# A fused attention and feed-forward block: dense work dealt to the attention steps in unequal shares, one diagonal to a part, values one step later

## The chip, the cores and the metric

The kernel runs on one core of a Trainium2 chip. The metric is the device time of one launch in microseconds (us). Three runs of the kernel before gave 3266.70, 3270.58 and 3273.54 us; their median is 3270.58.

## The reference

The input x has 16 batches of 512 tokens of width 512, in float32. Each batch passes through one block:

```python
a = attention(layernorm(x))           # 32 heads of width 16, biases, rotary positions, causal softmax
x = x + layernorm(a @ Wo.T + bo)
y = layernorm(x)
h = silu((y @ gate_w.T) * gate_s) * ((y @ up_w.T) * up_s)     # 1408 wide, weights are -1, 0 or 1
x = x + layernorm((h @ down_w.T) * down_s)
```

The layernorms have no parameters.

## The kernel before, in words

**Two strands in one program.** The attention is cut into head groups of four heads. A batch b has eight groups, and group n = 8b + g takes five *steps*, i = 0 to 4. After the attention matmuls of a step, a *share* of dense work is put into the program: projections, output projection, gate, up and down products, layernorms and transposes of the batch before and the batch after. `one_step` writes this order down. Each engine keeps the order of the program (`InOrder`), so the order written out is the order in which every engine's queue runs.

**A step of attention** (`one_step`, `scores`). A step issues two kinds of score matmuls into the two PSUM tiles `sc` (two heads in each):

- The transposed scores (keys on partitions) of group n, one part of `ST_PARTS`, go into the lower half. The row maxima are subtracted by a third matmul with `mx`. ScalarE takes the exponential of each tile into `pa` or `pc` (`weights`), and GpSimd clears the upper triangle of a diagonal block there.
- The plain scores (queries on partitions) of a group ahead, one part of `S_PARTS`, go into the upper half. VectorE adds a causal mask where the part holds a diagonal block, and reduces to the negated row maxima `nm` (`maxima`). Part = (i + 3) mod 5, so part 0 falls in step 2.

The two engines go through the tiles crosswise: ScalarE takes the first tile while VectorE takes the second, and then they change. The next step's scores write the same two tiles. In step 2 the finished maxima are transposed by TensorE (`turn_maxima`, PSUM tile `pm`) and split in two pieces (`nmh`, `nml`), which are written to `mx`.

**Values.** `values(n, 0)` multiplies the first weights `pa` (made in steps 0 and 1) by v, at the end of step 2 of the same group. `values(n, 1)` does the rest at the end of step 0 of the next group, and ScalarE copies the result out as `ot`. In a profile they are the matmuls `av`: 8 and 24 records.

**Dense work.** `dense`, `gate_ups` and `downs` build a list of items (cost, function). A float32 matmul costs `MM` = 1.0, an fp32r matmul `M1` = 0.27 and a transpose `TR` = 0.15; loads and vector work cost nothing. The functions are:

- `product`: a block of matmuls into one PSUM tile of a pool of three; the last matmul's item also calls the `tail`, which reads the tile on ScalarE or VectorE.
- `qk_block`: four matmuls; the tail makes `ys` (ScalarE, twice) and `ya` (VectorE), `rest` adds them (VectorE), makes the rounded piece `yh` (ScalarE) and the remainder `yl` (GpSimd). There is one buffer `ya`.
- `o_block`, `gate_up`, `down`: output projection (`po`), gate and up (`pg`, `pu`, each 8 fp32r matmuls) and down (`pd`, 22 fp32r matmuls to a token block). `split` makes the pieces `hh` (ScalarE) and `hl` (GpSimd) of the hidden values for the down product, with two buffers each; it stands in the list behind every eighth down matmul.
- `turn`: four transposes into one PSUM tile `px`.
- `merge` puts a piece of work in "after so many units of cost"; `laid` resolves this.

A full batch's list runs: v (16 matmuls), q (16), output projection (16), k (16) with transposes between, gate and up of 11 slices, and four down blocks with transposes. It has about 140 units for 40 steps. Batch 0 runs beside a shorter list (`first_list`, 46 steps, about one matmul a step), batch 14 beside one without down products, batch 15 beside a mixed one; the last dense work (`last_list`) has no attention beside it.

**How it is dealt out** (`run_list`). Each step takes items until the work done reaches an equal fraction of the total:

```python
goal = total * (s + 1) / steps
while i < len(L) and (done + L[i][0] / 2 < goal or s == steps - 1):
```

Loads are issued on SyncE's queue by items of the lists or by `later`.

Of the kernel before, what the change touches and what calls it, by code (L numbers as in the profile page):

```python
# [13 lines left out]
ALU = mybir.AluOpType  # L14
# [21 lines left out]

HALF = T // 2
ST_PARTS = [[(0, 0, 256, 0)], [(0, 256, 256, 0)], [(1, 128, 256, 0)], [(1, 384, 128, 0), (3, 384, 128, 128)], [(2, 256, 256, 0)]]
S_PARTS = [[(3, 0, 256, 0)], [(3, 256, 256, 0)], [(2, 0, 256, 0)], [(0, 0, 128, 0), (2, 256, 128, 128)], [(1, 0, 256, 0)]]
ST_DIAG = [0, None, 0, 128, 0]  # L40


class InOrder:
# [14 lines left out]
class Block:  # L58
# [54 lines left out]
    def constants(self):  # L113
        nc, a, con = self.nc, self.a, self.const
        for tb in range(NB):
            self.load_x(0, tb, ("x", "xr")[tb // 2], 2)
        ncol = sum(n for _, n in a["cols"][1])
        cols = con.tile([P, ncol], FP, tag="cols", name="cols")
        self.sp.dma_start(out=cols, in_=a["cols"][0])
        self.col, at = {}, 0  # L120
        for name, n in a["cols"][1]:
            self.col[name] = cols[:, at : at + n]
            at += n
        turn = con.tile([P, 2, T], FP, tag="turn", name="turn")
# [12 lines left out]
        self.row = {}  # L137
        for name in ("bo", "dscale"):
            self.row[name] = con.tile([P, C], FP, tag=name, name=name)
            nc.scalar.dma_start(out=self.row[name], in_=a[name].partition_broadcast(P))  # L140

        self.gh = con.tile([P, self.NF], FP, tag="gh", name="gh")
        self.gu = con.tile([P, self.NF], FP, tag="gu", name="gu")

        self.mask = con.tile([P, 2 * P], mybir.dt.bfloat16, tag="mask", name="mask")
        nc.gpsimd.memset(self.mask, 0.0)
        for i in range(2):
            m = self.mask[:, ts(i, P)]
            nc.gpsimd.affine_select(
                out=m, in_=m, compare_op=ALU.is_ge, fill=-BIG, base=0, pattern=[[-1, P]], channel_multiplier=1  # L150
            )
        self.sc = [self.ps_sc.tile([P, 2, T], FP, tag=f"sc{k}", name="sc") for k in range(2)]
        self.v17 = []
        for i in range(2):
            t = con.tile([P, NB, WIDTH], FP, tag=f"v17_{i}", name=f"v17_{i}")
            nc.gpsimd.memset(t, 0.0)
            nc.gpsimd.memset(t[:, :, DH : H * W : W], 1.0)
            self.v17.append(t)
        self.one = con.tile([P, P], FR, tag="one", name="one")
        nc.vector.memset(self.one.bitcast(FP), 1.0)  # L160
        self.qd, self.kd, self.od, self.rd = [], [], [], []
        for par in range(2):
            for c in range(NC):
# [110 lines left out]
        self.act.activation(out, src, AF.Identity, bias=mr[1], scale=mr[0])  # L274


    def turn(self, tiles, key, tb, to, big):

        st = {}

        def go(c):
            if c == 0:
                st["p"] = self.psum("px")
            self.pe.transpose(st["p"][:, ts(c, P)], tiles[key, tb][:, ts(c, P)], self.ident)
            if c == NC - 1:
# [12 lines left out]

        return [(TR, lambda c=c: go(c)) for c in range(NC)]

    def product(self, name, n, lhs, rhs, tail, cost=MM):
        st = {}

        def go(i):
            if i == 0:
                st["p"] = self.psum(name)
            self.pe.matmul(st["p"], lhs(i), rhs(i), start=(i == 0), stop=(i == n - 1))
            if i == n - 1:
                tail(st["p"])

        return [(cost, lambda i=i: go(i)) for i in range(n)]

    def norm_1(self, b, tb):
        xt = self.xts.pop((b, tb))
# [184 lines left out]
    def laid(items):  # L499
# [3 lines left out]
        for item in items:  # L503
# [2 lines left out]
                continue  # L506
            if item[0] == "need":
                for w in [w for w in waiting if w[2] == item[1]]:
                    out.append((0, w[1]))
                    waiting.remove(w)  # L510
                continue
            out.append(item)
            for w in waiting:
                w[0] -= item[0]
            for w in [w for w in waiting if w[0] <= 0]:
                out.append((0, w[1]))
                waiting.remove(w)
        return out + [(0, w[1]) for w in waiting]

    def dense(self, b, between=()):  # L520

# [105 lines left out]
    def maxima(self, m, part, s, two):  # L627
# [2 lines left out]
            self.nms[m] = self.tile([P, 2, 4, NB], "nm", bufs=2)  # L630
        full = self.nms[m]
        nm = full[:, :, two]
        if part in (1, 3, 4):
            d = s if part == 3 else s[:, :, P:HALF]
            mask = self.mask[:, 0 : d.shape[-1]].unsqueeze(1).to_broadcast(list(d.shape))
            self.dve.tensor_tensor(d, d, mask, ALU.add)
        out = [nm[:, 0, :, 3], nm[:, 1, :, 1], nm[:, 0, :, 2], nm[:, :, :, 0].rearrange("p x j -> p j x"), nm[:, 0, :, 1]][part]
        if part == 3:
            s = s.rearrange("p j (x t) -> p j x t", x=2)
        self.dve.tensor_reduce(out=out, in_=s, axis=AX.X, op=ALU.max, negate=True)  # L640
        if part == 4 and two.start == 0:
# [71 lines left out]
        self.later(2, lambda: self.pool.tensor_tensor(self.ocs[b, c], self.ocs[b, c], rc, ALU.mult))  # L713


    def run_list(self, L, steps):

        L = self.laid(L)
        total = sum(c for c, _ in L)
        done, i = 0.0, 0  # L720
        for s in range(steps):
            goal = total * (s + 1) / steps
            while i < len(L) and (done + L[i][0] / 2 < goal or s == steps - 1):
                L[i][1]()
                done += L[i][0]
                i += 1
            yield

    def gate_ups(self, o, nxt2, apart=False):
# [82 lines left out]
    def one_step(self, work, n, i):  # L812
# [5 lines left out]
        if i == 2 and 0 <= n + 1 < self.B * NG:  # L818
            self.turn_maxima(n + 1)
        next(work, None)  # L820
        if i == 2 and 0 <= n < self.B * NG:
            self.values(n, 0)
        if i == 0 and 0 <= n - 1 < self.B * NG:
            self.values(n - 1, 1)
# [2 lines left out]
    def front(self):  # L827
# [20 lines left out]
            return rest  # L848

        def turn(b, tb):  # L850
            for _, f in self.turn(self.xns, ("a", b), tb, self.xnts, ("xnta", "xntf")[b]):
                f()

        rest = None
# [14 lines left out]
        for name in "qk":  # L869
            for c in range(NC):  # L870
                items, rest, store = self.qk_block(0, name, c)
                for _, f in items[:2]:
                    f()
                for f in rests:
                    f()
                for _, f in items[2:]:
                    f()
                rests = [rest, store]
                if name == "q" and c == 0:
# [15 lines left out]
        nc.vector.tensor_scalar_mul(self.gh, self.col["gs"], 0.5)  # L895
        nc.vector.tensor_tensor(self.gu, self.gh, self.col["us"], ALU.mult)
        for tb in range(NB):
            for _, f in self.v_block(0, tb):
                f()
            if tb == 2:  # L900
                checks.pop(0)()
        for k in range(NC):
            self.wts[1, "v", k] = self.wts[0, "v", k]
        for tb in range(2):
            for _, f in self.v_block(1, tb):
                f()

    def first_list(self):
# [71 lines left out]

    def batches(self):
        B = self.B
        work = self.run_list(self.first_list(), 46)
        self.load_group(0)
        for n, i0 in ((-2, 2), (-1, 0)):
            for i in range(i0, STEPS):
# [16 lines left out]
        work = self.run_list(L + self.downs(B - 2, None, (0, 1), True, True), STEPS + 2)  # L1003
        for i in range(STEPS + 2):
            self.one_step(work, B * NG + i // STEPS, i % STEPS)
        for _, f in self.laid(self.last_list()):
            f()


# [59 lines left out]
```

## Time and profile before

| what | value |
|---|---|
| median of three runs | 3270.58 us |
| the profiled execution's own time | 3272.91 us |
| its span (first to last instruction) | 3271.1 us |
| PE (TensorE) busy | 3023.4 us, 92% |
| DVE (VectorE) busy | 2115.8 us, 65% |
| ACT (ScalarE) busy | 1607.1 us, 49% |
| POOL (GpSimd) busy | 1330.3 us, 41% |
| DMA queue of the loads and stores | 43.9% of 16 engines |
| mean granted TensorE clock | 0.979 |

Busy time is a union: matmuls overlap in the pipeline, so a busy PE is not an array at its peak. The number in a row of groups after "|" is the busy time and the mean of one instruction in ns, then the idle time of the engine just ahead of such instructions, and what ended it. In a timeline a row holds the start, the duration, engine, operation, output and inputs, the number of like instructions merged, and in brackets the idle time before them with what ended it. A float32 matmul of 512 columns appears as two records. All lines have the number L53, since a helper records every instruction; groups are told apart by the names of their tiles.

The timeline has batches 1 to 13 at 194 to 205 us each, batch 14 at 179 us. Before batch 0 the front part takes about 88 us, and the last dense work starts near 3140 us.

### The profile page before, as it was taken

Reading aid. Unit: us, or ns where it says so; the run is one execution under the profiler, and the core shown is the slowest. Engines: PE = TensorE matmul, PEld = TensorE weight load, DVE = VectorE, ACT = ScalarE, POOL = GpSimd, SP = SyncE. Lnnn points to the kernel's source line nnn. Section 1 sums busy time; section 2 is a strip of 40 time slices with the busy share of each in tenths; the row PEclk is TensorE's granted clock in tenths of the full one; section 3 lists DMA queues with packets and bytes.
Section 4 is the critical chain, followed back from the end, with each engine's and each line's share of the span. In section 5 each row is a group of like instructions: output and inputs, shape, how many; then the busy total and the mean of one; then the engine's idle time right before and its main releaser. Section 6 shows DMA issues by size and latency. Waiting matters only on the chain. (4 is left out here: it accounts for less than half of the span.)

```text
span 3271.1 us, 69062 instructions
## 1 busy us (share of the span) xinstructions
PE 3023.4 (92%) x26378; PEld 1812.4 (55%) x26378; DVE 2115.8 (65%) x3997; ACT 1607.1 (49%) x2758; POOL 1330.3 (41%) x1678
## 2 busy tenths in 40 slices
PE   6779999999999999999999999999999999999888
PEld 2334655646556464655646556464655646456556
DVE  5666657666676676667666676676657666576733
ACT  5354545454554544555454554544555454554432
POOL 4133344442544534344442444534344443443343
PEclk9989999999999999999999999999999999999999
DMA  7544535345453453535345453444535345343332
GB/s 254 170 152 148 189 100 161 126 149 167 129 160 116 152 163 122 188 103 162 128 153 160 134 168 104 151 159 127 189 104 167 122 147 168 114 146 122 125 101 72
DMA packets 271969, 472.04 MB, mean 144 GB/s; under 512 B 45920, under 2 KB 50016, under 8 KB 271200
## 3 DMA queue, kind: packets, MB, share of 16 engines
q1 hardware_dynamic: 271200, 466.49, 43.9%
q8 instruction: 212, 3.47, 0.4%
q14 instruction: 125, 1.02, 0.1%
q10 hardware_dynamic: 432, 1.05, 0.1%
HBM read 345.79 MB, written 125.30 MB: 144 GB/s over the span
## 5 line engine op out<-in xcount | busy, mean ns | idle before, releaser
L53 ACT ACTIVATE pa<-sc 128x512 f32<-128x512 f32 x1024 | 606.6, 597 | 795.7 <-PE sc L53 433.7
L53 DVE TENSOR_REDUCE nm<-sc 128x2 f32<-128x512 f32 (+1 forms) x1280 | 864.9, 689 | 158.1 <-PE sc L53 106.1
L53 DVE TENSOR_TENSOR sc<-sc,mask 128x256 f32<-128x256 f32 (+1 forms) x768 | 396.6, 516 | 476.3 <-PE sc L53 416.7
L53 POOL TENSOR_SCALAR_AFFINE_SELECT pa<-pa 128x512 f32<-128x512 f32 x384 | 244.9, 638 | 1022.8 <-ACT pa L53 698.5
L53 PEld LDWEIGHTS sc<-kh,q 32*128 32x128 f32 x3072 | 154.2, 185 | 492.7 <-issue 142.3
L53 PE MATMUL sc<-kh,q 32*128 32x256 f32 (+1 forms) x3072 | 276.5, 357 | 119.3 <-DVE nm L53 97.4
L53 PE MATMUL pd<-wd,hl 128*128 128x512 f32 x704 | 291.1, 413 | 24.9 <-POOL hl L53 24.9
L53 POOL TENSOR_TENSOR hl<-ht,hh 128x512 fp32r<-128x512 f32 (+1 forms) x192 | 229.6, 1196 | 200.0 <-ACT hh L53 199.9
L53 PE MATMUL pd<-wd,hh 128*128 128x512 f32 x704 | 291.0, 413 | 2.3 <-ACT hh L53 2.3
L53 PE MATMUL pg<-xntf,wf 128*128 128x512 f32 x704 | 286.2, 406 | 2.7 <-ACT xntf L53 2.7
L53 PE MATMUL pg<-xntfl,wf 128*128 128x512 f32 x704 | 283.3, 402 | 0.7 <-DVE xntfl L53 0.7
L53 PE MATMUL pu<-xntfl,wf 128*128 128x512 f32 x704 | 282.8, 402 | 0.0
L53 PE MATMUL pu<-xntf,wf 128*128 128x512 f32 x704 | 282.5, 401 | 0.0
L53 PE MATMUL av<-pa,v 128*32 128x512 f32 (+2 forms) x3072 | 281.8, 470 | 0.0
L53 POOL TENSOR_TENSOR yl<-ya,yh 128x512 fp32r<-128x512 f32 x128 | 163.2, 1275 | 219.7 <-ACT yh L53 219.7
L53 POOL TENSOR_TENSOR ln_rstd<-ln_ve,neghalf 128x1 f32<-128x1 f32 x256 | 142.6, 557 | 266.2 <-DVE ln_ve L53 266.0
L53 PE MATMUL pk<-xnta,w 128*128 128x512 f32 x480 | 243.9, 636 | 1.5 <-DVE ya L53 1.5
L53 PE MATMUL po<-w,oc 128*128 128x512 f32 x512 | 240.9, 608 | 2.5 <-DMA w<-in_wo 2.5
L53 PE MATMUL pq<-xnta,w 128*128 128x512 f32 x480 | 231.8, 618 | 6.4 <-ACT xntf L53 5.8
L53 ACT CAST hh<-ht 128x512 fp32r<-128x512 f32 (+1 forms) x192 | 111.5, 581 | 250.5 <-PE pd L53 199.3
L53 PE MATMUL sc<-mx,one 2*128 2x256 f32 (+1 forms) x3072 | 225.6, 278 | 4.1 <-DMA mx<-nml 3.9
L53 PE MATMUL sc<-q,kh 32*128 32x256 f32 (+1 forms) x3072 | 225.2, 278 | 0.3 <-DVE nm L53 0.3
(123 smaller groups left out, 5398.6 us busy)
## 6 DMA issues: line engine op xcount, KB each, us to landing
wf<-wgs SPq DMA_DIRECT2D x352, 256.0 KB
q<-qd SPq DMA_DIRECT2D x128, 256.0 KB
kh<-kd SPq DMA_DIRECT2D x128, 256.0 KB
kl<-kd SPq DMA_DIRECT2D x128, 256.0 KB
od<-ot SPq DMA_DIRECT2D x128, 256.0 KB
w<-in_wo SPq DMA_DIRECT2D x68, 256.0 KB
xr<-in_x SPq DMA_DIRECT2D x66, 256.0 KB
w<-in_wq SPq DMA_DIRECT2D x64, 256.0 KB
```

The costliest lines, as they stand in the source:

```text
L53: return self.tc.keep_in_program_order(f(*args, **kwargs))
```

## The change

It does four things.

- **Unequal shares.** `SHARES` gives the five steps the weights 2.3, 3.8, 3.8, 2.4 and 3.5 (sum 15.8) instead of equal ones. `first` says at which step a list begins (2 for the first list).
- **Where a share ends.** Among the places near its goal the one with the lowest score is taken: distance from the goal, plus 0.8 for each unit that the end lies nearer than one unit behind the last matmul of a block. A merged piece of work counts as half a unit behind. Of equal scores the earliest counts, so items without cost that stand at the end of a share fall to the next one.
- **One diagonal a part.** Part 2 of `S_PARTS` now holds the two small blocks (query block 0 on its diagonal, query block 2 with its first 128 keys) and part 3 holds query block 2 with the next 256 keys. Every part but part 0 has just one diagonal block, and `S_DIAG` tells where it lies. Before, part 3 had two diagonals (a 512-wide mask), parts 1 and 4 had one, parts 0 and 2 none. The mask tile shrinks to one block.
- **Values.** The first lot goes from step 2 to step 3.

```diff
-S_PARTS = [[(3, 0, 256, 0)], [(3, 256, 256, 0)], [(2, 0, 256, 0)], [(0, 0, 128, 0), (2, 256, 128, 128)], [(1, 0, 256, 0)]]
+S_PARTS = [[(3, 0, 256, 0)], [(3, 256, 256, 0)], [(0, 0, 128, 0), (2, 0, 128, 128)], [(2, 128, 256, 0)], [(1, 0, 256, 0)]]
+S_DIAG = [None, 128, 0, 128, 128]
+SHARES = [2.3, 3.8, 3.8, 2.4, 3.5]
...
-        return [(TR, lambda c=c: go(c)) for c in range(NC)]
+        return [(TR, lambda c=c: go(c), *[0.0] * (c == NC - 1)) for c in range(NC)]
...
-        return [(cost, lambda i=i: go(i)) for i in range(n)]
+        return [(cost, lambda i=i: go(i), *[0.0] * (i == n - 1)) for i in range(n)]
...
-                out.append((0, w[1]))
+                out.append((0, w[1], 0.5))
...
-        if part in (1, 3, 4):
-            d = s if part == 3 else s[:, :, P:HALF]
-            mask = self.mask[:, 0 : d.shape[-1]].unsqueeze(1).to_broadcast(list(d.shape))
-            self.dve.tensor_tensor(d, d, mask, ALU.add)
+        at = S_DIAG[part]
+        if at is not None:
+            d = s[:, :, at : at + P]
+            self.dve.tensor_tensor(d, d, self.mask.unsqueeze(1).to_broadcast(list(d.shape)), ALU.add)
...
-        if part == 3:
+        if part == 2:
             s = s.rearrange("p j (x t) -> p j x t", x=2)
...
-    def run_list(self, L, steps):
+    def run_list(self, L, steps, first=0):
...
-        total = sum(c for c, _ in L)
-        done, i = 0.0, 0
+        total = sum(item[0] for item in L)
+        weights = [SHARES[(first + s) % STEPS] for s in range(steps)]
+        done, i, goal = 0.0, 0, 0.0
         for s in range(steps):
-            goal = total * (s + 1) / steps
-            while i < len(L) and (done + L[i][0] / 2 < goal or s == steps - 1):
-                L[i][1]()
-                done += L[i][0]
-                i += 1
+            goal += total * weights[s] / sum(weights)
+            best, end, at, since = None, i, done, 9.0
+            for k in range(i, len(L) + 1):
+                score = abs(at - goal) + 0.8 * max(0.0, 1.0 - since)
+                if best is None or score < best:
+                    best, end = score, k
+                if k == len(L) or at > goal + 2.0:
+                    break
+                cost, _, *tail = L[k]
+                at += cost
+                since = min(since + cost, *tail, 9.0)
+            if s == steps - 1:
+                end = len(L)
+            for item in L[i:end]:
+                item[1]()
+                done += item[0]
+            i = end
             yield
...
-        if i == 2 and 0 <= n < self.B * NG:
+        if i == 3 and 0 <= n < self.B * NG:
             self.values(n, 0)
...
-        work = self.run_list(self.first_list(), 46)
+        work = self.run_list(self.first_list(), 46, 2)
```

More of the change, by code (lines that the diff above doesn't have):

```diff
@@ L143, in constants @@
         self.gu = con.tile([P, self.NF], FP, tag="gu", name="gu")
[L145 to L151, printed above, removed]
+        m = self.mask = con.tile([P, P], mybir.dt.bfloat16, tag="mask", name="mask")
+        nc.gpsimd.memset(m, 0.0)
+        nc.gpsimd.affine_select(
+            out=m, in_=m, compare_op=ALU.is_ge, fill=-BIG, base=0, pattern=[[-1, P]], channel_multiplier=1
+        )
         self.sc = [self.ps_sc.tile([P, 2, T], FP, tag=f"sc{k}", name="sc") for k in range(2)]
@@ L515, in laid @@
             for w in [w for w in waiting if w[0] <= 0]:
-                out.append((0, w[1]))
+                out.append((0, w[1], 0.5))
                 waiting.remove(w)
-        return out + [(0, w[1]) for w in waiting]
+        return out + [(0, w[1], 0.5) for w in waiting]
     def dense(self, b, between=()):
@@ L632, in maxima @@
         nm = full[:, :, two]
-        if part in (1, 3, 4):
-            d = s if part == 3 else s[:, :, P:HALF]
-            mask = self.mask[:, 0 : d.shape[-1]].unsqueeze(1).to_broadcast(list(d.shape))
-            self.dve.tensor_tensor(d, d, mask, ALU.add)
-        out = [nm[:, 0, :, 3], nm[:, 1, :, 1], nm[:, 0, :, 2], nm[:, :, :, 0].rearrange("p x j -> p j x"), nm[:, 0, :, 1]][part]
-        if part == 3:
+        at = S_DIAG[part]
+        if at is not None:
+            d = s[:, :, at : at + P]
+            self.dve.tensor_tensor(d, d, self.mask.unsqueeze(1).to_broadcast(list(d.shape)), ALU.add)
+        out = [nm[:, 0, :, 3], nm[:, 1, :, 1], nm[:, :, :, 0].rearrange("p x j -> p j x"), nm[:, 0, :, 2], nm[:, 0, :, 1]][part]
+        if part == 2:
             s = s.rearrange("p j (x t) -> p j x t", x=2)
@@ L850, in turn @@
         def turn(b, tb):
-            for _, f in self.turn(self.xns, ("a", b), tb, self.xnts, ("xnta", "xntf")[b]):
+            for _, f, *_ in self.turn(self.xns, ("a", b), tb, self.xnts, ("xnta", "xntf")[b]):
                 f()
@@ L871, in front @@
                 items, rest, store = self.qk_block(0, name, c)
-                for _, f in items[:2]:
+                for _, f, *_ in items[:2]:
                     f()
@@ L875, in front @@
                     f()
-                for _, f in items[2:]:
+                for _, f, *_ in items[2:]:
                     f()
@@ L897, in front @@
         for tb in range(NB):
-            for _, f in self.v_block(0, tb):
+            for _, f, *_ in self.v_block(0, tb):
                 f()
@@ L904, in front @@
         for tb in range(2):
-            for _, f in self.v_block(1, tb):
+            for _, f, *_ in self.v_block(1, tb):
                 f()
@@ L1005, in batches @@
             self.one_step(work, B * NG + i // STEPS, i % STEPS)
-        for _, f in self.laid(self.last_list()):
+        for _, f, *_ in self.laid(self.last_list()):
             f()
```

## The prediction

> **What bounds the kernel now.** I read the page's busy shares first (PE 92%), then the forty slices (PE at 9 from the fourth to the 37th), then the groups kept apart by shape, the waits, and the timeline of one batch (1043 to 1239 us). TensorE is the bound, so only its idle time and slow-clock time can be won. Below, "g.i" is step i of head group g of a batch.
>
> The scores of a step overwrite the score PSUM, so they may start only when the step before has been read out. What that needs, from the groups by shape (busy, mean ns | idle, its causes):
>
> ```profile
> L53 DVE TENSOR_REDUCE nm<-sc 128x2 f32<-128x512 f32 x1024 | 687.6, 688 | 149.4 <-PE sc L53 106.1 <-ACT pc L53 23.6 <-ACT y L53 0.7
> L53 ACT ACTIVATE pa<-sc 128x512 f32<-128x512 f32 x1024 | 606.6, 597 | 795.7 <-PE sc L53 433.7 <-DVE nm L53 338.0 <-PE pu L53 4.8
> ...
> L53 DVE TENSOR_TENSOR sc<-sc,mask 128x256 f32<-128x256 f32 x512 | 218.9, 427 | 355.6 <-PE sc L53 317.9 <-ACT pa L53 34.4 <-ACT ot L53 2.3
> ...
> L53 DVE TENSOR_TENSOR sc<-sc,mask 128x512 f32<-128x512 f32 x256 | 177.7, 694 | 120.8 <-PE sc L53 98.9 <-ACT pa L53 11.3 <-ACT yh L53 9.6
> ```
>
> VectorE works through two halves, so its **need** from the end of the scores, with 0.4 us before its first instruction, is 1.75 us without a mask, 2.65 with a 256-wide one (2 x (0.43 + 0.69) + 0.4) and 3.15 with the 512-wide. The **cover** is what PE does meanwhile. From starts in the timeline: 0.86 us per f32 matmul of 512 (two records of 0.43), 0.23 per fp32r one, 0.11 per transpose, 0.40 for the two changes of kind, and for values 1.03 (first lot) or 1.43 (second). Step 1.3, 8 records: 8 x 0.43 + 0.40 = 3.84 us of cover, against this timeline of TensorE:
>
> ```profile
> 1081.65 3.70 PE L53 MATMUL pq<-xnta,w 128*128 128x512 f32 x8
> 1086.01 0.39 PE L53 MATMUL sc<-kh,q 32*128 32x256 f32 x4 [0.66 <-DVE nm L53]
> ...
> 1086.81 2.84 PE L53 MATMUL po<-w,oc 128*128 128x512 f32 x6
> 1090.90 0.36 PE L53 MATMUL sc<-kh,q 32*128 32x128 f32 x4 [1.25 <-DVE nm L53]
> ```
>
> The need was 4.5, not 2.65. Why, the same timeline for VectorE says, here at step 3.2:
>
> ```profile
> 1124.30 0.68 DVE L53 TENSOR_TENSOR ya<-ya,ys 128x512 f32<-128x512 f32 x1
> 1127.14 0.75 DVE L53 SCALAR_TENSOR_TENSOR ya<-pk,cols,turn 128x512 f32<-128x512 f32 x1 [2.16 <-POOL yl L53]
> ```
>
> The end of one q or k block (`rest`) and the tail of the next stand side by side on VectorE: the second waits 2.16 us for ScalarE's yh and GpSimd's yl, and the next maxima wait behind it. TensorE meets this a second time, in the transpose of the maxima, which needs the PSUM slot that this tail frees:
>
> ```profile
> 1127.94 0.28 PE L53 MATMUL pm<-ident,nm 128*16 128x128 f32 x1 [2.40 <-DVE ya L53]
> ```
>
> In the down product the exponentials of step 7.3 stand behind a split (`hh`) that waits for matmuls of the same step:
>
> ```profile
> 1231.91 0.51 ACT L53 CAST hh<-ht 128x384 fp32r<-128x384 f32 x1 [5.71 <-PE pd L53]
> ```
>
> Waits of batches 2 to 13 by step, us: 1.3 0.73, 1.4 1.32, 2.3 0.96 (a transpose), 3.2 2.17, 3.3 0.62, 3.4 0.90, 7.2 and 7.3 together 3.6, 7.4 0.7. That is 11.0 a batch; the whole gate and up part (4.0 to 6.4) has none. A batch takes 193.9 when the clock stays up (the eleventh), 196.0 on average.
>
> **What the Trainium skill says.** "PSUM — Partial Sum Buffer", *Engine vs sequencer instructions*: the queues of ScalarE, VectorE and GpSimd are strict FIFO. The 5.71 us above agree: exponentials whose scores were ready stood behind hh. The same page, *PSUM bank collisions*: two engines must be kept off one bank; here the second exponential waits for the first reduce (338.0 us in the group above). "TensorE: Matmul & The Clock Gate", *What's actually happening*: the array falls to half rate after an idle window of about 3.4 us. Here shorter waits suffice: after 1.6 and 0.4 us of waiting in 7.2 the granted clock was 0.51:
>
> ```profile
> 1226.00:1229.40 3.40, 3.40 (x37) 1.73 (x40) 1.14 (x4) 0.20 (x1) 3.40 (x4) 0.51 0.21 80
> ```
>
> Between 255 and 2985 us it fell so 15 times, mostly after 3.2 or 7.2, at about 2 us each.
>
> **The change part by part.**
> *Masks.* A group's masks cost 4 x 427 + 2 x 694 = 3.10 us before, 8 x 427 = 3.42 after, +41 us of VectorE over 128 groups. It is 65% busy: free wherever the cover exceeds the need, counted below where it does not. Needs become 2.65, 2.65, 1.75, 2.65, 2.65 for steps 0 to 4. The extra 128-wide score pieces go from step 0 to step 4 (scores 0.80 us instead of 0.59), no net time. Two GpSimd instructions fewer in the constants: nothing.
> *Values a step later.* Four matmuls (8 records), no DMA. Their exponentials ended two steps before; the `pa` buffer they free is wanted two steps on. Cost nothing, cover is the interval itself; without it the PE would wait for the exponentials of step 1 only.
> *Shares.* The same work, so no PE time. Full batch covers in the gate part become about 3.9, 4.1, 4.1, 3.5, 3.8 against 3.4 in the barest step before; nothing waited there, so nothing is won. Items without cost at a share's end now fall to the next share: loads issue about 0.7 us later on SP's queue. PE waited for kh, kl, mx and w some 18 us in all, so I take 0 (-2 to +6).
>
> *q blocks.* Order after: 1.0 two matmuls ending a block, 1.1 five, 1.2 four, 1.3 two, 1.4 four. From the end of 1.0's scores, VectorE by the durations above: maxima 1.1 to 6.8; block (add 0.85, yh 0.62, yl 1.28, tail 0.67) to 10.6; maxima 1.2 to 11.9; block to 16.15; maxima 1.3 to 18.3. TensorE would be ready at 17.3: wait 1.1. Step 1.4 then covers its own (3.84). 1.1 for 2.05, less what the scores shift: **-0.9**.
> *k blocks.* After: 3.1 and 3.2 again hold an end and a tail each, and between the maxima of 3.1 and the add stands the statistics of x1 (0.69 + 0.18 + 0.15). The tail ends at 16.5, TensorE is at the transpose by 13.4: wait 3.0 for 2.17; 3.3 0.35 for 0.62; 3.4 none for 0.90, but its k block's tail now leads into 4.0, which covers 3.9 of 4.7: 0.85. With three gate matmuls fewer in the stretch and the longer scores of 2.4: **+0.8**.
> *Down product.* Same order on ScalarE. 7.2 loses its values (cover down 1.03), 7.3 gains them: exponentials behind hh end the need at 4.7 against 3.8, wait 0.9 for 1.6. In 7.2 GpSimd's hl is late by 0.95 for 1.2, but the transpose then waits for xn 1.4 for 0.4. 7.0 gets 0.35. Sum **0**.
> 13 full batches: 13 x (-0.9 + 0.8 + 0) = -1.3.
> *Batch 14* has no down product, covers of 2.9 in steps 1 and 3 and about 11 us of waits; with 3.3 or more everywhere I take back 4, the q and k loops stay. *Batch 15* has covers of 2.1 to 2.5 in steps 1 and 3 (0.3 to 1.9 late, ten times, 6.2 us); after, 2.5 to 3.2: 1.5 remain, -4.7. *First 46 steps*: one matmul a step, the need sets them: -0.5 in step 0, -0.5 in step 2 (no values), +0.9 in step 4: 0 (-6 to +6).
> *Clock.* The longer pm wait: a little more often at half rate, +3 (-10 to +12).
>
> Sum: 3272.9 (span 3271.1 and 1.8 around it) - 1.3 - 4 - 4.7 + 3 = 3265.9. The profiled run lies 2.3 above the median of the three, so 3264 as a median. A measurement of this kernel tells about 0.2%, 6.5 us, from no change.
>
> **Rivals.**
> *The waits dissolve.* If in 1.1, 3.1 and 3.2 the tail finds yl ready, because the longer share lets it arrive later, two of three 2.16 us blocks vanish: about 3 us a batch, 40 over 13, with their clock losses: 3225. For it: 3.2 has four matmuls instead of three. Against: the add is queued behind the maxima either way.
> *The k wait grows and the clock follows; slower.* The pm transpose in 3.2 costs 3.0 by my working; if x1's statistics come later still, 3.8, and if both long waits then cost a half-rate stretch nearly every batch (26 for 13, 2 us each), 13 x 0.8 + 26 = +35: 3297. It decides from the point where q no longer gives back 0.8 a batch.
> *Short steps run out.* Steps 0 and 3 rest on values; 16 a batch, each 0.25 us short gives 4 us, 52 in all: 3316. Against: their cover exceeds the need by 0.8.
> *No effect*: every wait keeps its size, 3270.
>
> **Numbers.** Likeliest 0.45, own range 3248 to 3280 (faster 0.26, same 0.11, slower 0.08 of it); dissolve 0.26; clock and pm 0.21, short steps 0.05; no effect 0.03, of which 0.02 same. Faster 0.53, same 0.13, slower 0.34. Range 3220 to 3302.
>
> **What would show it.** Right: 1.3 waits about 1.1 us and 1.4 nothing; pm waits for ya near 3 us; 7.3 still behind hh; gate steps without waits; the 512-wide mask row gone and 1024 of 256. Wrong: yl waits on VectorE falling from 134 us by half, or VectorE waits for scores in gate steps.

## The result and the profile after

The changed kernel takes 3298.08 us (median of 7 runs, 3289.97 to 3310.59) against 3270.58 in the same session (7 runs): ratio 1.0091, 95% interval 1.0069 to 1.0114. It is **slower by 0.9%**; the forecast was 3264. The profiled execution of the changed kernel took 3305.37 us, span 3303.5 (before: 3272.91, span 3271.1), so the traces differ by 32.4 us, a little more than the medians.

Where the 32.4 us lie, by stretches of the two traces. A batch begins here with the score matmuls of step 0 of its first group, and batch 15 is taken to the scores of its last step. In brackets, how long TensorE had half its clock:

| stretch | before, us (half clock) | after, us (half clock) | difference |
|---|---|---|---|
| up to batch 0 | 108.9 (10.2) | 112.3 (17.1) | +3.4 |
| batch 0 | 147.3 (30.2) | 165.5 (56.5) | **+18.3** |
| batch 1 | 198.8 (10.7) | 198.2 (8.4) | -0.7 |
| batches 2 to 13 | 2351.9 (51.2) | 2364.7 (58.0) | **+12.8** |
| batch 14 | 178.6 (10.2) | 179.3 (6.8) | +0.7 |
| batch 15 | 158.5 (13.7) | 155.1 (10.2) | -3.5 |
| end | 126.9 (14.0) | 128.3 (16.9) | +1.4 |

The 205 us given above for the longest batch count the last two steps of batch 0 into batch 1; by these boundaries batches 1 to 13 take 194 to 199 us before.

The groups by shape after (busy, mean ns | idle before, its causes):

```profile
L56 DVE TENSOR_REDUCE nm<-sc 128x2 f32<-128x512 f32 x1024 | 699.6, 692 | 113.4 <-PE sc L56 86.5 <-ACT pa L56 0.3
L56 ACT ACTIVATE pa<-sc 128x512 f32<-128x512 f32 x1024 | 607.0, 598 | 783.6 <-PE sc L56 409.0 <-DVE nm L56 347.0 <-PE pu L56 7.6
L56 DVE TENSOR_TENSOR sc<-sc,mask 128x256 f32<-128x256 f32 x1024 | 437.2, 427 | 469.0 <-PE sc L56 396.8 <-ACT pa L56 56.1 <-ACT pc L56 11.1
```

The 512-wide mask is gone, and 1024 masks of 256 cost 437.2 us where both kinds cost 396.6 before: the +41 us of VectorE that were counted. The durations did not change; the waits did. TensorE's waits between 450 and 2985 us (in total, times, longest), before:

```profile
PE sc L53 <- DVE nm L53: 64.0, 71, 2.4
PE pm L53 <- DVE ya L53: 25.1, 12, 2.4
PE px L53 <- ACT xn L53: 17.7, 35, 1.3
```

and after:

```profile
PE px L56 <- ACT xn L56: 35.8, 40, 1.8
PE pm L56 <- DVE ya L56: 34.1, 12, 3.0
PE sc L56 <- DVE nm L56: 33.1, 50, 2.3
...
PE sc L56 <- ACT hh L56: 7.0, 25, 0.3
PE pg L56 <- DVE ya L56: 5.9, 12, 0.5
```

This is the answer in small for the full batches. Scores waiting for maxima, which unequal shares and later values address, fell from 64.0 to 33.1 us. The 31 us came back elsewhere: transposes waiting for `xn` +18.1, the transpose of the maxima +9.0, and 12.9 us of two waits that were not there. The first of these is no work of the new dealing: with the new masks and later values under the old dealing (an experiment below) transposes wait 35.0 us for `xn` already.

The steps shown before, now in batch 5. TensorE from step 1.3 on:

```profile
1105.53 1.98 PE L56 MATMUL pq<-xnta,w 128*128 128x512 f32 x4
1107.44 1.06 PE L56 MATMUL av<-pa,v 128*32 128x512 f32 x8
1109.24 0.33 PE L56 MATMUL sc<-kh,q 32*128 32x128 f32 x4 [0.73 <-DVE nm L56]
...
1111.21 2.74 PE L56 MATMUL po<-w,oc 128*128 128x512 f32 x6
1113.88 0.39 PE L56 MATMUL sc<-kh,q 32*128 32x256 f32 x4
```

Step 1.3 waits 0.73 us and 1.4 no more, where the prediction had 1.1 and none. Step 3.2, VectorE and then TensorE:

```profile
1147.98 0.68 DVE L56 TENSOR_TENSOR ya<-ya,ys 128x512 f32<-128x512 f32 x1
1150.82 0.75 DVE L56 SCALAR_TENSOR_TENSOR ya<-pk,cols,turn 128x512 f32<-128x512 f32 x1 [2.16 <-POOL yl L56]
```

```profile
1151.62 0.28 PE L56 MATMUL pm<-ident,nm 128*16 128x128 f32 x1 [2.94 <-DVE ya L56]
```

The end of one k block and the tail of the next still stand side by side with the 2.16 us between them, and the transpose of the maxima waits 2.94 us. From here on such a pair is called a **join**. By VectorE's order a full batch has six of them in both kernels, in 1.1, 1.2, 1.3, 3.1, 3.2 and 3.3 before and in 1.1, 1.2, 1.4, 3.1, 3.2 and 3.4 after. In the down product ScalarE still has the split ahead of the exponentials:

```profile
1254.97 0.51 ACT L56 CAST hh<-ht 128x384 fp32r<-128x384 f32 x1 [3.12 <-PE pd L56]
```

### The profile page after: what moved, and what is told of

Its sections match the earlier page's. It is cut to its first block, busy times and chain, and to the rows that moved or that the text cites. A ratio compares the mean times of both kernels' runs of the same rounds, so it can differ in the third digit from the quotient of the medians.

```text
span 3303.5 us, 69520 instructions
## 1 busy us (share of the span) xinstructions
PE 3036.6 (92%) x26378; PEld 1813.2 (55%) x26378; DVE 2168.4 (66%) x4253; ACT 1602.6 (49%) x2758; POOL 1326.7 (40%) x1677
## 5 line engine op out<-in xcount | busy, mean ns | idle before, releaser
L56 DVE TENSOR_REDUCE nm<-sc 128x2 f32<-128x512 f32 (+1 forms) x1280 | 877.0, 692 | 122.2 <-PE sc L56 86.5
L56 DVE TENSOR_TENSOR sc<-sc,mask 128x256 f32<-128x256 f32 x1024 | 437.2, 427 | 469.0 <-PE sc L56 396.8
L56 PE MATMUL pd<-wd,hl 128*128 128x512 f32 x704 | 283.9, 403 | 24.7 <-POOL hl L56 24.7
L56 ACT ACTIVATE pc<-sc 128x512 f32<-128x512 f32 x256 | 151.4, 597 | 302.2 <-PE sc L56 175.3
L56 PE MATMUL pk<-xnta,w 128*128 128x512 f32 x480 | 259.4, 667 | 4.1 <-DVE ya L56 4.1
```

Of the source, the lines that this page charges most:

```text
L56: return self.tc.keep_in_program_order(f(*args, **kwargs))
```

## What was new: items that fall behind the next step's queue

The new rule takes the end of a share with the smallest score, and among equals the first. An item without cost leaves the distance to the goal as it is, so it never improves the score: the laid items that follow a share's last matmul always fall to the next share. The old rule took them along whenever the work done was still short of the goal. In the program the next share stands behind the next step's scores, so a fallen item stands **behind the next step's maxima on VectorE and behind its exponentials on ScalarE**. In a full batch this moved little against the kernel before: the end of the last q block went from 1.4 to 2.0, and the last of the four `xn` from 3.1 to 3.2. One step looks like a case of it and is none; the cases are in batch 0.

*Step 2.3.* ScalarE in batch 11, after:

```profile
2312.91 0.60 ACT L56 ACTIVATE pa<-sc 128x512 f32<-128x512 f32 x1 [1.79 <-PE sc L56]
2315.27 0.60 ACT L56 ACTIVATE pa<-sc 128x512 f32<-128x512 f32 x1 [1.76 <-DVE nm L56]
2315.76 0.80 ACT L56 ACTIVATE xn<-x,ln_sh,ln_rstd 128x512 f32<-128x512 f32 x1
```

TensorE, and the stretch after it (busy of PE, PEld, DVE, ACT, POOL, then the granted clock):

```profile
2316.62 0.55 PE L56 MATMUL px<-ident,xn 128*128 128x128 f32 x3 [1.83 <-ACT xn L56]
```

```profile
2319.00:2323.00 4.00, 4.00 (x32) 2.74 (x33) 2.44 (x6) 1.42 (x3) 2.19 (x4) 0.50 0.74 200
```

`xn` runs 4.0 us after the scores of its step began, behind both exponentials, the second of which waited for the maxima. The transposes wait 1.83 us for it, and then the clock is halved. But `xn` stood in 2.3 behind the same two exponentials in the kernel before. ScalarE and TensorE there, in batch 11:

```profile
2283.23 0.60 ACT L53 ACTIVATE pa<-sc 128x512 f32<-128x512 f32 x1 [0.70 <-DVE nm L53]
2283.72 0.80 ACT L53 ACTIVATE xn<-x,ln_sh,ln_rstd 128x512 f32<-128x512 f32 x1
```

```profile
2284.58 0.66 PE L53 MATMUL px<-ident,xn 128*128 128x128 f32 x4 [0.77 <-ACT xn L53]
```

With the values alone moved and all dealing as before (an experiment below), the wait is nearly that of the changed kernel:

```profile
2261.43 0.66 PE L53 MATMUL px<-ident,xn 128*128 128x128 f32 x4 [1.60 <-ACT xn L53]
```

Without the values in 2.2 the scores of 2.3 come 1.0 us earlier, while VectorE still has statistics to make ahead of its maxima. So the second exponential and `xn` behind it wait longer. In batches 2 to 13 the steps 2.3 and 2.4 took 12.15 us on average after, 8.85 before: 1.0 us is the values' matmuls that moved into 2.3, 1.1 this wait, and 1.1 half clock. The wait has no single cause, as two experiments below shorten it with the values left late. That ScalarE's and VectorE's queues let nothing pass is what the Trainium skill says ("PSUM — Partial Sum Buffer", *Engine vs sequencer instructions*: strict FIFO), and this trace agrees: GpSimd had the last input of `xn` ready at 2313.4 us, and ScalarE stood idle for 1.76 us ahead of the exponential in front of it.

*Batch 0.* VectorE and TensorE, after:

```profile
141.88 0.93 DVE L56 TENSOR_TENSOR ya<-ya,ys 128x512 f32<-128x512 f32 x1
144.96 0.75 DVE L56 SCALAR_TENSOR_TENSOR ya<-pq,cols,turn 128x512 f32<-128x512 f32 x1 [2.15 <-POOL yl L56]
```

```profile
142.97 1.07 PE L56 MATMUL av<-pa,v 128*32 128x512 f32 x8
147.99 0.48 PE L56 MATMUL sc<-kh,q 32*128 32x128 f32 x4 [3.95 <-DVE nm L56]
```

With one matmul a step, the old dealing had put a block's end into one step and the next block's tail into the next, with the maxima between them. Now the end falls to the step of the tail. VectorE's order up to the end of batch 0 has 6 joins where it had 1 (the expectations below say 5 and leave out the one in step 7.2). Here the next scores wait 3.95 us behind one, and the matmuls after it run at half clock (0.48 us for 0.33).

## The experiments

Ratios are to runs of the kernel before on the same chip (its medians there 3273.5 to 3275.4 us). "A batch" is the mean over batches 2 to 13 in the profiled run; before has 195.99 us, the changed kernel 197.06. The expectations give batch 0 about 146 us before and 167 after, from boundaries that hold 40 steps in the one and 41 in the other; the results below use those of the table, 147.3 and 165.5.

### Which part of the change costs

**The first list dealt as before** (`run_even` is the old `run_list`; it serves only the list beside batch 0):

```diff
-        work = self.run_list(self.first_list(), 46, 2)
+        work = self.run_even(self.first_list(), 46)
```

> The changed kernel with one thing undone: the first list (46 steps beside batch 0) is dealt as before, in equal shares with the old rule for their ends; masks, values and the shares of all other lists stay changed. Joined theory (in the first list the end of a q or k block now falls into the share of the next block's tail, so VectorE waits 2.2 us for GpSimd there and the maxima behind it): the stretch from the start of batch 0 to batch 1 goes back from 167 us to about 146, total 3277. Mask theory (the first list is set by VectorE's need, and the added masks lengthened it whatever the dealing): no change, 3298.

Measured: 3287.73 us, ratio 1.0045 (1.0031 to 1.0060), and batch 0 falls from 165.5 to 143.2 us. Half of the loss is the first list's dealing.

**The reverse:** the kernel before, with the first list alone dealt by the new rule and shares.

```diff
-        work = self.run_list(self.first_list(), 46)
+        work = self.run_list(self.first_list(), 46, 2)
...
-                work = self.run_list(L, NG * STEPS)
+                work = self.run_even(L, NG * STEPS)
```

> The kernel before with one thing added: the first list is dealt by the new rule with the unequal shares; masks, values and all other lists as before. Joined theory: the stretch of batch 0 grows from 146 us to about 165, total 3290. Mask theory: 146, total 3271.

Measured: 3287.83 us, ratio 1.0037 (1.0024 to 1.0050), batch 0 161.0 us where the kernel before has 147.3. Nearly the same loss without new masks and without later values: it is the dealing.

**Masks and values, all dealing as before:**

```diff
-        work = self.run_list(self.first_list(), 46, 2)
+        work = self.run_even(self.first_list(), 46)
...
-                work = self.run_list(L, NG * STEPS)
+                work = self.run_even(L, NG * STEPS)
```

> The kernel before with one diagonal to a part and the first values a step later, but every list dealt as before. Joined theory: the first list stays at about 146 us; full batches change by what the masks and the moved values do alone, -0.5 to +1 us each, total 3265 to 3285. Mask theory: batch 0 takes about 165 us, total 3290 or more.

Measured: 3300.03 us, ratio 1.0067 (1.0044 to 1.0091), batch 0 143.3 us, a batch 197.78. Batch 0 stays short, as expected, but the full batches lose 1.8 us each. There was a second cause, and it had to be split. This run and the first differ only in how the later lists are dealt, and the new dealing has the lower ratio (1.0045 against 1.0067). The intervals overlap, so a gain is not shown, but neither is a loss: as far as these runs show, what the new dealing costs, it costs in the first list.

**Masks alone** (on the kernel before: new `S_PARTS`, `S_DIAG` and `maxima`; values in step 2):

```diff
-S_PARTS = [[(3, 0, 256, 0)], [(3, 256, 256, 0)], [(2, 0, 256, 0)], [(0, 0, 128, 0), (2, 256, 128, 128)], [(1, 0, 256, 0)]]
+S_PARTS = [[(3, 0, 256, 0)], [(3, 256, 256, 0)], [(0, 0, 128, 0), (2, 0, 128, 128)], [(2, 128, 256, 0)], [(1, 0, 256, 0)]]
+S_DIAG = [None, 128, 0, 128, 128]
```

> The kernel before with the new masks alone (one diagonal in each of the score parts 1 to 4, none of 512 columns); dealing of the dense work and the step of the values as before. In the run with parts and values together the clean batch was 1.9 us longer and the waits in step 1.4 grew from 1.32 to 2.17 us. Theory A (the masks cost: step 4 now needs 2.65 us of VectorE where 1.75 were enough, and it is the step behind a joined end and tail): batches 1.0 to 1.9 us longer, the start of batch 0 5 us later, batch 0 some 4 us shorter, 3285 to 3298. Theory B (the masks are free as the prediction had them and the values cost): 3267 to 3277.

Measured: 3328.24 us, ratio **1.0180** (1.0127 to 1.0234), a batch 199.41. Even above theory A's range.

**Values alone** (on the kernel before):

```diff
-        if i == 2 and 0 <= n < self.B * NG:
+        if i == 3 and 0 <= n < self.B * NG:
```

> The kernel before with the first lot of values one step later alone. Theory A (the later values are cover for step 3, whose waits of 0.7 us in 1.3 and 0.6 in 3.3 and 1.6 in 7.3 they shorten, and step 2 does without): 1.0 to 1.5 us less a batch, 3250 to 3262. Theory B (step 2 runs short of cover without them and the loss of parts and values together comes from here): 3285 to 3300.

Measured: 3236.54 us, ratio **0.9880** (0.9855 to 0.9904), a batch 193.96. It gains more than either theory had. The two parts add up: +1.80 - 1.20 = +0.60%, and together they measured +0.67%.

Where the values gain is seen at the end of step 7.3. Before, the last matmul of the share, `pd`, is followed by this wait; with the values there, by the second:

```profile
2407.31 0.39 PE L53 MATMUL sc<-kh,q 32*128 32x256 f32 x4 [1.53 <-DVE nm L53]
```

```profile
1410.39 1.06 PE L53 MATMUL av<-pa,v 128*32 128x512 f32 x8
1411.97 0.39 PE L53 MATMUL sc<-kh,q 32*128 32x256 f32 x4 [0.52 <-DVE nm L53]
```

Step 7.2 loses the same matmuls and gains no wait: those it had (1.18 for `hl`, 0.45 for `xn`) stood ahead of the values and stay as they were. Group 7 falls from 27.98 to 26.61 us, group 3 from 27.21 to 26.15, and group 2 rises by 0.8, since the wait in 2.3 grows from 0.77 to 1.60 us.

Where the masks cost is step 1.4 of the run with masks alone:

```profile
1312.18 2.84 PE L56 MATMUL po<-w,oc 128*128 128x512 f32 x6
1317.09 0.39 PE L56 MATMUL sc<-kh,q 32*128 32x256 f32 x4 [2.06 <-DVE nm L56]
...
1317.88 5.40 PE L56 MATMUL po<-w,oc 128*128 128x512 f32 x8
```

Step 1.4 went from 4.89 to 5.94 us; then the same eight records as in 2.2 of the trace after (3.60 us there) take 5.40, because the clock is halved: 2.0 went from 6.09 to 7.08. VectorE comes late to 1.4 because a join stands ahead of its maxima. Steps 2.4, 3.4 and 7.4 lost 0.5 to 0.8 each, and 3.2 lost 0.9 with twice the half clock.

**The mask of step 4 left out** of the run with masks alone:

```diff
-S_DIAG = [None, 128, 0, 128, 128]
+S_DIAG = [None, 128, None, 128, 128]
```

> The run with the new masks alone, with the mask of step 4 left out (the two diagonals of that score part are not masked, so this part of the computation is missing; 512 instructions of VectorE fewer over the groups than with it: 256 adds of 256 columns, 109 us of VectorE's time). Theory A (the masks cost because step 4 now needs 2.65 us of VectorE and stands behind a joined end and tail in 1.4 and 3.4, with a stretch of half clock after 1.4): the loss goes, 3255 to 3275. Theory B (the loss comes from the other steps, or from the pieces of scores that moved from step 0 to step 4, 0.2 us each): 3305 to 3330.

Measured: 3257.16 us, ratio 0.9960 (0.9944 to 0.9975), and 1.4 back at 4.89. This run also has less to mask than the kernel before, 0.53 us less to a group in step 0. So it doesn't price the mask of step 4 alone, but with that mask out nothing of the loss is left.

### Which part of the dealing costs

**Laid items kept with the share that they end**, else the changed kernel:

```diff
+            while end < len(L) and L[end][0] == 0 and L[end][2:] == (0.5,):
+                end += 1
             if s == steps - 1:
                 end = len(L)
```

> The changed kernel with one line added: after the end of a share is chosen, merged work of no cost that stands right behind it (the ends of q and k blocks, x1 and y work) stays in that share, so that it is issued before the next step's scores; unequal shares, masks and values stay. In the first list the add then stands before the maxima and the tail behind them. Joined theory: batch 0 falls from 167 us to about 148, and in full batches two of six joined pairs (steps 1.4 and 3.4) come apart, -0.5 to -1 us each: total 3262 to 3280. Theory that the uneven counts of matmuls in a step (none, one or two) make the loss: 3295 to 3300.

Measured: 3243.59 us, ratio **0.9894** (0.9868 to 0.9920), a batch 193.28. Two lines turn the change from 0.9% slower to 1.1% faster; 54.5 us lie between the medians. A full batch has four joins instead of six, batch 0 none. Steps 2.3 and 2.4 fall from 12.15 to 9.15, because ScalarE now has `xn` ahead of the exponentials, where it stood in neither kernel. So this is more than a loss undone:

```profile
2069.10 0.81 ACT L56 ACTIVATE xn<-x,ln_sh,ln_rstd 128x512 f32<-128x512 f32 x1 [1.89 <-POOL ln_sh L56]
2069.82 0.57 ACT L56 ACTIVATE pa<-sc 128x512 f32<-128x512 f32 x1
```

**The block's end laid a matmul earlier**, else the changed kernel:

```diff
-            self.merge(L, rest, 3)
+            self.merge(L, rest, 2)
```

> The changed kernel with the end of a q or k block (ya + ys) laid after 2 instead of 3 matmuls of the next block; shares, end rule, masks, values as changed. In VectorE's order the joins of an end with the next block's first instruction fall from 6 to 4 a batch and from 5 to 0 beside batch 0, as in the run that keeps the laid items with their share. Joined theory: as that run, 3238 to 3254. Rival (a matmul earlier, ys is not there yet, and the addition waits with the maxima behind it): 3270 to 3300.

Measured: 3247.91 us, ratio 0.9938 (0.9908 to 0.9968), a batch 194.13, batch 0 146.6 us. This leaves shares, rule, masks and values alone and moves only the ends of blocks; four joins are left in a full batch and none in batch 0. `xn` stays behind the exponentials of 2.3, but VectorE comes to that step earlier, and the wait for `xn` falls from 1.83 to 0.84 us. In batch 0, VectorE and TensorE:

```profile
137.56 0.69 DVE L56 TENSOR_TENSOR ya<-ya,ys 128x512 f32<-128x512 f32 x1
...
141.63 0.75 DVE L56 SCALAR_TENSOR_TENSOR ya<-pq,cols,turn 128x512 f32<-128x512 f32 x1 [1.19 <-PE sc L56]
```

```profile
144.66 0.33 PE L56 MATMUL sc<-kh,q 32*128 32x128 f32 x4 [2.15 <-DVE nm L56]
```

The tail finds `yl` done and waits for TensorE only; the scores wait 2.15 us where they waited 3.95.

**Equal shares**, else the changed kernel:

```diff
-SHARES = [2.3, 3.8, 3.8, 2.4, 3.5]
+SHARES = [1.0] * 5
```

> The changed kernel with the five shares made equal; the rule for a share's end, the masks and the step of the values stay as changed. VectorE's order then has as many ends of a block (ya + ys) right before the next block's first instruction as the changed kernel has: 6 a full batch, 5 in batch 0. Joined theory (the end rule is what costs, in batch 0): within 6 us of the changed kernel, 3290 to 3304. Share theory (the unequal shares give back 1 to 2 us a batch in steps 1, 2 and 4): 3310 to 3325.

Measured: 3288.02 us, ratio 1.0052 (1.0035 to 1.0070), a batch 194.56, batch 0 168.6. Both theories were wrong about the unequal shares, which seem to cost rather than to give. How much is less sure: the ratios differ by 0.4%, about 13 us, and the intervals just touch. The profiled runs differ by 2.5 us a batch (7.04 against 9.14 us in 3.2, 4.90 against 6.45 in 7.2), of which half-clock time explains 1.6, but this run's profile is of the fastest of its eight executions and the changed kernel's of one above its median.

**Kept items and the old first list together**, against the changed kernel:

```diff
+            while end < len(L) and L[end][0] == 0 and L[end][2:] == (0.5,):
+                end += 1
...
-        work = self.run_list(self.first_list(), 46, 2)
+        work = self.run_even(self.first_list(), 46)
```

> The changed kernel with both repairs: the first list (beside batch 0) dealt as before, and elsewhere the items without cost that are laid into a block kept with the share that they end. Joined theory: batches as in the run that keeps them (median 193.2 us), batch 0 142 us instead of 158, start 2 us later: 3226 to 3234. Rival (batch 0's gain and the later batches' gain are one and the same slack, or the clock takes it): 3240 to 3250.

Measured: 3240.01 us, ratio 0.9890 (0.9856 to 0.9923), not distinguishable from keeping alone. Batch 0 took 157.2 us where the same order of instructions took 143.2 in the first experiment; TensorE was at half clock for 61.6 us against 18.5. Batch 0's time in one profile is thus no measure of 14 us.

**Laid items kept on the kernel before** (written into its old rule; this takes one join apart and also moves `xn` from 2.3 to 2.2):

```diff
                 i += 1
+            while i < len(L) and L[i][0] == 0 and L[i][2:] == (0.5,):
+                L[i][1]()
+                i += 1
             yield
```

> The kernel before, with its own masks, equal shares and values, and one edit: items without cost that are laid at a share's end stay with that share. In VectorE's order of a full batch this takes apart only one join, that of steps 3.1 and 3.2 (the addition moves ahead of the maxima of 3.2), beside batch 0 only the last one. Joined theory: the wait of the transpose of the maxima (2.17 us of 3.2) and its half clock (1.7 us of it a batch, 0.85 us of time) go: 3.0 us a batch less, 3228 to 3245. Rival (the statistics of x1, which stand in the same steps on VectorE, hold the tail back as well, so the wait stays): 3262 to 3275.

Measured: 3256.16 us, ratio 0.9953 (0.9934 to 0.9973). That lies between the two theories. The wait of the transpose fell from 25.1 to 7.4 us over twelve batches, so it hung on the join. But 3.0 and 3.1 grew by 0.47 and 0.95 us, since the addition now stands behind the statistics of x1 and ahead of the maxima of 3.1, and the half clock in 3.2 stayed (1.99 us a batch). The gain was 1.15 us a batch instead of 3.0, and little of it is the join's: group 3 as a whole gained 0.2 us, group 2 gained 0.5, where the wait of 2.3 went from 0.77 to 0.01, and group 7 gained 0.65, where half clock fell from 2.56 to 0.85 us.

### A better version

**Old masks** in the kernel with kept items and the old first list (values later, unequal shares); `maxima` and the mask tile are those of before:

```diff
-S_PARTS = [[(3, 0, 256, 0)], [(3, 256, 256, 0)], [(0, 0, 128, 0), (2, 0, 128, 128)], [(2, 128, 256, 0)], [(1, 0, 256, 0)]]
-S_DIAG = [None, 128, 0, 128, 128]
+S_PARTS = [[(3, 0, 256, 0)], [(3, 256, 256, 0)], [(2, 0, 256, 0)], [(0, 0, 128, 0), (2, 256, 128, 128)], [(1, 0, 256, 0)]]
```

> The changed kernel with the old masks, the first list dealt as before, and the laid items kept with the share that they end: against the run e8_keep_first_even only the masks are undone. If the masks cost here what they cost alone (3.4 us a batch): 3185 to 3200. Half of it, since 1.4 has no wait left here and only 2.4, 3.4 and 7.0 have: 3205 to 3222. Rival (with the joins gone step 4's cover suffices and the masks are free): 3234 to 3246.

Measured: 3215.30 us, ratio 0.9838 (0.9809 to 0.9867), 0.5% less than with the new masks (17 us by the ratios, 25 by the medians).

**And equal shares as well:**

```diff
-SHARES = [2.3, 3.8, 3.8, 2.4, 3.5]
+SHARES = [1.0] * 5
```

> As f3_old_masks_keep with equal shares: old masks, values a step later, the rule for a share's end with laid items kept, the first list as before. If equal shares are worth what they were in the changed kernel (about 2.5 us a batch, of it 1.6 through the clock): 25 to 35 us below f3. If with the joins gone the shares do not matter: within 8 us of f3. Theory of one slack (each repair takes the same waits): 3225 to 3240, no better than the values alone.

Measured: **3189.14 us, ratio 0.9747** (0.9721 to 0.9772), a batch 190.42, 3.4 us of half clock in all of batches 2 to 13 where before had 51.2. It is 2.5% faster than the kernel before. A share's end now lies between the two halves of the join that stood in 3.1, as it does with the items kept on the kernel before. VectorE and TensorE there:

```profile
1288.98 0.68 DVE L55 TENSOR_TENSOR ya<-ya,ys 128x512 f32<-128x512 f32 x1
...
1293.29 0.75 DVE L55 SCALAR_TENSOR_TENSOR ya<-pk,cols,turn 128x512 f32<-128x512 f32 x1 [0.38 <-POOL oc L55]
```

```profile
1294.10 0.28 PE L55 MATMUL pm<-ident,nm 128*16 128x128 f32 x1 [0.64 <-DVE ya L55]
```

The maxima of 3.1 run between the two, `yl` is done in their time, and step 3.2 takes 4.78 us where it took 8.32 before, of which 1.0 is the values that moved on, and 9.14 after with a longer share.

**And the block's end a matmul earlier in it:**

```diff
-            self.merge(L, rest, 3)
+            self.merge(L, rest, 2)
```

> f4_best_guess with the end of a q or k block laid after 2 instead of 3 matmuls of the next block: one join fewer in a full batch (3 instead of 4), and no join is left beside batch 0. Joined theory: another 0.5 to 1 us a batch and some 3 us in batch 0, 3172 to 3184. Rival (the waits left in 1.3 and 7.3 are set elsewhere, and the addition now waits for ys): 3186 to 3200.

Measured: 3189.85 us, ratio 0.9753 (0.9717 to 0.9789): no further gain. The rival holds; a batch (190.26) keeps its waits for `hl` in 7.2 and for the maxima in 1.3.

## Why the prediction was wrong, step by step

- **The steps that failed: masks "free wherever the cover exceeds the need", values "Cost nothing".** Alone they measured +1.80% (59 us) and -1.20% (39 us), together +0.67%, which is 22 us of the loss. *Masks:* the need of 2.65 us in step 4 was right. But it counts from the end of the scores, and VectorE doesn't begin there: in 1.4 it comes late by a join, and the wait grows from 1.25 to 2.09 us, with half clock after it. In the changed kernel 1.4 itself does not wait, as predicted, since its share is longer; undoing the masks still brought 17 to 25 us with the items kept. *Values:* the working had the gain in 7.3 (1.6 to 0.9 us; alone 1.53 to 0.52) and set two waits of 7.2 against it, which did not grow. The step it left out is 2.3, whose transposes wait for `xn`: its 0.96 us stand in the list of waits and in none of the sums. As the masks' loss and the values' gain are near each other, the sum hid both.
- **And "First 46 steps: ... 0 (-6 to +6)".** The dealing of the first list alone cost 0.37% on the kernel before and, undone, gave back 0.46% (12 and 15 us); in the traces batch 0 has +18.3 us, of which half clock explains 13, (56.5 - 30.2) / 2. The sum counted needs and covers and not what order the new rule gives there. That the six joins are what costs is argued. Dealt anew with its joins, batch 0 took 161.0 to 168.6 us in three runs; dealt anew without them 146.6 and 156.4; dealt as before 142.4 to 157.2 in nine. These are single profiles.
- **"Items without cost at a share's end now fall to the next share: loads issue about 0.7 us later on SP's queue ... so I take 0".** The fall was seen, but only loads were counted; the ends of q and k blocks fall too. In batch 0 this made the joins. In the full batches six stayed six, and the dealing of all later lists measured -0.22%, no loss. That keeping the items gives 54.5 us (64 by the two ratios) is a gain that the rule left lying, not what it cost against the kernel before.
- **q blocks -0.9, k blocks +0.8, down product 0.** Right. TensorE's waits over 0.1 us, by batch: in group 1 they fell from 1.91 to 0.75 us, in 3.0 to 4.0 they rose from 3.50 to 4.24, in group 7 from 3.29 to 3.45. What is missing is group 2: 0.79 to 1.88, and half clock that costs 1.1 more.
- **Batch 15 -4.7** measured -3.5. **Batch 14 -4** measured +0.7; its cause was not followed up.
- **Clock +3 (-10 to +12).** Half-clock time rose by 33.6 us in the span, a cost of 17; batch 0 alone rose by 26.2. In batches 1 to 14 it stayed (72.2 and 73.2).
- **The signs named.** 1.4, the transpose near 3 us, the split, the gate steps and the mask rows came out as written, 1.3 at 0.75 us for 1.1; VectorE's waits for `yl` fell to 122.9 us, not by half. They describe the parts that were right and none tested the fall. The rival "the k wait grows and the clock follows" had nearly the right number, 3297 (its sum 13 x 0.8 + 26 is 36, not 35), by a mechanism that gave only a part: the transpose's wait grew by 0.7 us a batch and half clock in 3.2 from 1.7 to 2.6, but the clock of the full batches as a whole did not follow.

What stays open: how much the unequal shares cost and why, what in the first list's order costs, and the 0.1% that the parts (masks and values +0.67, first list +0.37, the other lists -0.22) lack to +0.91.

## What to carry to other kernels

When a rule deals work to slots, ask of every item without cost on which side of a boundary it ends: on strict queues, a boundary is a place behind the next slot's reads, whatever the item's price. A stage's slack is not the mean of its engine: 41 us more on a VectorE that is 65% busy cost 59 us, because they lay in steps where that engine was already late. And where matmuls are moved, ask what else they gave time to: the values moved for step 3's scores had also covered the transposes of 2.3. Of a change with several parts, try each alone; here one part lost 1.8%, one gained 1.2%, the dealing of one list lost 0.4%, and two lines about items without cost were worth 2%.

## What was not expected of the hardware

- TensorE's clock is halved after shorter waits than the Trainium skill gives ("TensorE: Matmul & The Clock Gate", *What's actually happening*: an idle window of about 3.4 us). Here it was 0.50 from 2317.2 us on for 6.8 us, after one wait of 1.83 us in 2.3, and a wait of 2.06 us in 1.4 was followed by eight records in 5.40 us instead of 3.60. The same wait does not always bring it: in batches 2 to 13, 2.3 had it in five after the change, and in none with equal shares, where it waits 1.83 us as well. The same page's *A second HAM failure mode* tells of short idle times between groups of matmuls that bring the clock down; it tells of another kernel and gives no length, but it is nearer to what these traces show.
- The same instructions in the same order took 143.2 and 157.2 us in batch 0 of two runs, at half clock for 18.5 and 61.6 us.
